# A graph network with an eigensolver on one core: a norm's small steps moved from VectorE to GpSimd, and a residual add made by a copy and an accumulating DMA

## The chip, the core and the metric

The kernel runs on one core of one Trainium2 chip. The core has five engines with a queue each: TensorE (PE; its weight loads are PEld), VectorE (DVE), ScalarE (ACT), GpSimd (POOL) and SyncE (SP, which here only issues DMAs). An engine takes its instructions in the order of the program; a semaphore wait at the head of a queue holds all that stands behind it. The metric is the time in microseconds of one execution on the device. One execution of each kernel was also taken by the hardware profiler.

## The reference, cut to what matters

x has 64 batches of 256 rows and 256 features; adj is 256 x 256. All is float32.

```python
h = maximum(layernorm(x), 0)                    # layer 0
g = adj * adj
t = relu(g @ (h @ W1))                          # 256 -> 512, per batch
t = relu(g @ (t @ W2))                          # 512 -> 1024
x = x + g @ (t @ W3)                            # 1024 -> 256
h = maximum(layernorm(x), 0)                    # layer 1
L = normalised laplacian of adj
U = eigenvectors of L (eigh)
h = relu((U.T @ h) @ W1' + b1)                  # 256 -> 128
x = x + U @ (h @ W2' + b2)                      # 128 -> 256
```

with `layernorm(x) = (x - mean) / sqrt(var + 1e-5)` over the features.

## The kernel before, in words

Two jobs run beside each other. The **eigen chain** (class `Eigen`) finds U: a Householder reduction to tridiagonal form of 254 steps, 16 small QL problems, four merge levels (32, 64, 128, 256). Almost all of it is small VectorE instructions that depend on each other, with a square root on ScalarE, transposes on TensorE and, in the first half of the reduction, up to nine small instructions of a step on GpSimd (named m, q, qn, qs, none, gg, gu, xc in the profile; `aside` chooses GpSimd while `lo < P` and VectorE after it; m and none stay on GpSimd to the end).

**Layer 0** (class `Layers`) has no need of U. It goes over 32 pairs of batches. For pair q: `begin` loads x (two DMAs of 256 KB) and makes `norm` and `relu_norm`, which give h0; `first` to `fourth` are the matrix products, whose results ScalarE takes out of PSUM; `last` multiplies with g once more and adds x, which gives x1, a tile of 128 partitions x 1024 (two 128 x 512 halves, m = 0 and 1). x1 of the first 30 pairs is spilled to DRAM by SyncE, that of the last two is kept (`KEPT = 2`). `norm1` normalises x1 into h1, `turn_rows` transposes it, `for_layer1` multiplies it with the first weight of layer 1 and spills the product.

A float32 product appears in the trace as two matmul instructions.

`norm` takes for each of the four rows of a partition: a Copy on ScalarE with a running sum, one VectorE instruction for minus the mean (nm), a Square on ScalarE with a running sum (v); then for the four together one VectorE scaling of v, a square root on ScalarE, a reciprocal, a correction step of three, a reciprocal and the shift, all on VectorE. In all seven small VectorE instructions. `relu_norm` applies scale and shift in four ScalarE instructions.

**Layer 1** (`layer1`) needs U and goes over the pairs again, in three stages of a software pipeline (`to_vectors`, `from_vectors`, `finish`), twelve products in all for a pair. GpSimd adds x1 and the bias product (xb, two instructions of 128 x 512 for a pair).

The **order** on every engine is fixed when the program is built, by a planner (`Pace`). It keeps a clock for each engine and a price for each instruction (`Op`: `busy` is how long the engine is taken, `until` when the result can be read). The eigen chain is written out in its own order; before each of its instructions, `Pace.chain` asks when that instruction is due and `Pace.run` puts in front of it those instructions of the two layer-0 streams (`products` and `rows`) which by their prices start earlier. A matmul that would go past the due time is cut in two. Chain instructions are priced 6% longer than their nominal price (13% while the QL problems run), layer-0 ones at their nominal price. So TensorE is given layer-0 products until the chain's next transposes are due, and real times that differ from the prices show up as waits at the head of a queue.

The two streams are each in order. `rows` gives begin(0), begin(1), norm1(0), begin(2), norm1(1) and so on. `products` gives, for pair q: third(q), turn_rows(q-1), half of fourth(q), for_layer1(q-1), first(q+1), the other half of fourth(q), second(q+1), last(q). norm1(q) thus has third(q+1) to hide under. The last pair's turn_rows waits until layer 1 says so: layer 1 starts with the planner weaving what is left of layer 0 between its own instructions (there one layer-0 product goes ahead of about each layer-1 product), and when it comes to its ninth pair (`LAST_AT = 12`, three pairs ahead) everything left of layer 0 is put in at once (`pace.finish`), since pairs 30 and 31 come twelfth and thirteenth in its order.

The small pools matter for the edit: x has two buffers, x1 two, and the PSUM pool of layer 0 has four banks, which `bank()` hands out in turn.

In the profile nearly every instruction carries line 209, the line of the planner that issues it (213 when the planner no longer weaves), so the tiles tell what an instruction is. `x<-x,bank` is the residual add, `junk<-x` a Copy of a norm, `junk<-x,nm` its Square, `s<-v` its square root, `h<-x,shift,scale` relu_norm, `s<-bank` and `y<-bank` evictions of products, `p<-bank` one of fourth, `p,gt` the products of last, `gt,h` those of first, `eye,h` those of turn_rows, `ident,ac` the chain's transposes. x1 and x are one name in it, and so are `L_gnn_W` of both layers.

Of the kernel before, what the change touches and what calls it, by code (L numbers as in the profile page):

```python
# [21 lines left out]
F32 = mybir.dt.float32  # L22
AF = mybir.ActivationFunctionType
OP = mybir.AluOpType
# [3 lines left out]
N = 256  # L28
P = 128
# [6 lines left out]
LN_EPS = 1e-5  # L36
# [46 lines left out]
class Op:  # L83
# [4 lines left out]
    def __init__(self, part, call, args, kwargs):  # L88
        self.part, self.engine, self.call, self.args, self.kwargs = part, ENGINES[part], call, args, kwargs
        self.name = call.__name__  # L90
        free = lambda a: int(np.prod([int(n) for n in a.shape[1:]]))
        named = dict(kwargs)
        outs = [named.pop("out")] if "out" in named else [args[0]]
        ins = [a for a in [*(args if "out" in kwargs else args[1:]), *named.values()] if isinstance(a, bass.AP)]
        total = named.pop("accum_out", None)
        if isinstance(total, bass.AP):
            outs.append(total)
            ins = [a for a in ins if a is not total]
        self.outs, self.ins = [span(a) for a in outs], [span(a) for a in ins]
        n = max(free(a) for a in outs[:1] + ins) if self.engine == "DVE" else free(outs[0])  # L100
        sums = len(outs) > 1

        if self.engine == "PE":
            self.columns = 0 if "transpose" in self.name else n
            self.busy = max(n * self.COLUMN, 0.224) if self.columns else 0.115
            self.until = max(self.busy, 0.165) + 0.35
        elif self.engine == "ACT":
            pointers = any(isinstance(kwargs.get(k), bass.AP) for k in ("scale", "bias"))
            self.busy = 0.13 + n / 1400 + 0.12 * pointers + 0.19 * sums
            self.until = self.busy + 0.12  # L110
        elif self.engine == "DVE":
            each = 6.3 if self.name == "reciprocal" else 2.0 if self.name == "tensor_tensor_scan" else 1.0
            pointers = self.name == "scalar_tensor_tensor" or any(a.shape[1:] == [1] for a in ins[1:])
            self.busy = 0.065 + 0.06 * pointers + each * n / 960 + 0.08 * sums
            self.until = self.busy + 0.125
        elif self.engine == "POOL":
            self.busy = 0.2 + 2 * n / 960
            self.until = self.busy + 0.1
        else:
            self.busy, self.until = 0.1, 4.0  # L120
# [13 lines left out]
def span(a):  # L134

    step = a.ap[0][0]
    lo = a.offset % step if step else a.offset
    return a.tensor.name, lo, lo + sum((int(n) - 1) * abs(int(s)) for s, n in a.ap[1:]) + 1
# [142 lines left out]
class Eigen:  # L281
# [998 lines left out]
    def level(self, n, qt, dc, rho, sg, bad=None):  # L1280
# [93 lines left out]
        def spread(ps, column):  # L1374

            for h in range(H):
                nc.tensor.matmul(
                    ps if last else ps[:, seg[h]],
                    lhsT=column[:, h : h + 1].to_broadcast([P, P]),
                    rhs=perm[:, h, :],  # L1380
                    start=h == 0 or not last,
                    stop=h == H - 1 or not last,
                )
# [349 lines left out]
class Layers:  # L1733


    def __init__(self, tc, ctx, ap, gt2, u, ut):
        self.tc, self.nc, self.ap = tc, tc.nc, ap
        self.gt2, self.u, self.ut = gt2, u, ut
        pool = ctx.enter_context(tc.tile_pool(name="layers", bufs=1))
        self.kept = ctx.enter_context(tc.tile_pool(name="kept", bufs=KEPT))  # L1740
        dram = ctx.enter_context(tc.tile_pool(name="dram", bufs=1, space=bass.MemoryType.DRAM))
        self.x1, self.hw = {}, {}
        self.x, self.h0, self.y1, self.y2, self.s2, self.p3, self.h1, self.new = ({} for _ in range(8))
        self.begun, self.rows_of = set(), {}
        self.due = False
        self.spilled = {
            q: dram.tile([P, H * 2 * N], F32, name=f"x1_{q}") for q in range(PAIRS - KEPT)
        }
        self.spilled_hw = {
            q: dram.tile([P, H * 2 * P], F32, name=f"hw_{q}") for q in range(PAIRS - KEPT)  # L1750
        }
        self.w = {}
        for name in ("L0_gnn_W1", "L0_gnn_W2", "L0_gnn_W3", "L1_gnn_W1", "L1_gnn_W2"):
            rows, cols = ap[name].shape
            self.w[name] = pool.tile([P, rows // P, cols], F32, name=name)
        self.b1 = pool.tile([P, P], F32, name="b1")
        self.eye = pool.tile([P, P], F32, name="eye")
        self.b2 = pool.tile([P, N], F32, name="b2")
        self.u1 = pool.tile([P, H], F32, name="u1")
        self.ub2 = pool.tile([P, H, N], F32, name="ub2")  # L1760

    def load_weights(self):
        dma, ap = self.nc.sync.dma_start, self.ap
        for name, t in self.w.items():
            dma(out=t, in_=ap[name].rearrange("(c p) n -> p c n", p=P))
        dma(out=self.eye, in_=ap["c_mats"][0][0:P, 0:P])
        for b, t in (("L1_gnn_b1", self.b1), ("L1_gnn_b2", self.b2)):
            dma(out=t, in_=ap[b].rearrange("(o n) -> o n", o=1).to_broadcast(list(t.shape)))
# [42 lines left out]
    def norm(self, x, scale, shift, parts=range(4)):  # L1811

        nc = self.nc
        g = H * 2
        at = slice(parts[0], parts[-1] + 1, parts[1] - parts[0])
        s, nm, v, tmp = (self.sp.tile([P, g], F32, tag=c, name=c) for c in ("s", "nm", "v", "tmp"))
        for j in parts:
            junk = self.sp.tile([P, N], F32, tag="junk", name="junk", bufs=1)
            yield nc.scalar.activation(junk, x[:, j // 2, j % 2, :], AF.Copy, accum_out=s[:, j : j + 1])
        yield nc.vector.tensor_scalar(nm[:, at], s[:, at], -1.0 / N, None, OP.mult)  # L1820
        for j in parts:
            junk = self.sp.tile([P, N], F32, tag="junk", name="junk", bufs=1)
            yield nc.scalar.activation(
                junk, x[:, j // 2, j % 2, :], AF.Square, bias=nm[:, j : j + 1], accum_out=v[:, j : j + 1]
            )
        s, nm, v, tmp, scale, shift = (t[:, at] for t in (s, nm, v, tmp, scale, shift))

        yield nc.vector.tensor_scalar(v, v, 0.25 / N, 0.25 * LN_EPS, OP.mult, OP.add)
        yield nc.scalar.activation(s, v, AF.Sqrt)
        yield nc.vector.reciprocal(tmp, s)  # L1830
        yield nc.vector.tensor_tensor(tmp, tmp, v, OP.mult)
        yield nc.vector.tensor_tensor(s, s, tmp, OP.add)
        yield nc.vector.reciprocal(scale, s)
        yield nc.vector.tensor_tensor(shift, nm, scale, OP.mult)

    def relu_norm(self, x, scale, shift, h, parts=range(4)):
        for j in parts:
# [34 lines left out]
    def rows(self):  # L1872

        for q in range(PAIRS + 1):
            if q < PAIRS:
                if q > 0:
                    yield lambda: q - 1 in self.begun
                yield from self.begin(q)
            if q > 0:
                yield lambda: q - 1 in self.new  # L1880
                yield from self.norm1(q - 1)
# [101 lines left out]
    def last(self, q):  # L1983

        nc, x, p3 = self.nc, self.x.pop(q), self.p3.pop(q)
        x1 = self.kept.tile([P, H, 2, N], F32, tag="x1", name="x1")
        for m in range(H):
            ps = self.bank()
            yield from self.products_of(ps, [(self.gt2[:, h, m * P : (m + 1) * P], p3[:, h, :]) for h in range(H)])
            yield nc.vector.tensor_tensor(flat(x1)[:, m, :], flat(x)[:, m, :], ps, OP.add)  # L1990
        if q in self.spilled:
            yield nc.sync.dma_start(out=self.spilled[q], in_=x1.rearrange("p h b f -> p (h b f)"))
        else:
            self.x1[q] = x1
        self.new[q] = x1
# [137 lines left out]
def flat(t):  # L2133
    return t.rearrange("p h b f -> p h (b f)")
# [63 lines left out]
```

## Time and profile before

| | us |
|---|---|
| median of 3 runs (2427.26 to 2429.52) | 2429.36 |
| span of the profiled execution | 2426.6 |
| TensorE idle before layer-0 products that wait for ScalarE (s), whole run | 6.5 |
| ScalarE idle before relu_norm, waiting for shift, 50 times | 54.4 |
| ScalarE idle before the square root of a norm, waiting for v, 47 times | 36.8 |
| ScalarE idle before Square, waiting for nm, 42 times | 32.6 |
| GpSimd idle before m, waiting for the eigen chain's xr, 250 times | 526.5 |
| DMA queue of SyncE, share of 16 engines | 10.8% |

TensorE's clock was granted in full (0.999 on the mean). The longest chain of work that the profile follows back from the end starts only at 2247.6 us, where U is done; from there it is TensorE's products of layer 1 with one pair's norm in front. The rest of the reading is in the prediction, with its lines.

How to read the views: a group's row has the operation, the tiles out<-in, the shapes, the count, then busy us and mean ns of one, then idle time before it and who ended it. A row of a tile's view has the count and the shortest, median and longest duration in ns. A row of waits has the total us, the number of times and the longest. A row of the timeline has the start, the length, the engine, the operation and, in brackets, the idle time before it.

### The profile page before, as it was taken

The numbers are of one execution on the slowest core, as the hardware profiler recorded it, in microseconds if no ns is written. First come the engines' busy times: TensorE is split into PE (matmuls) and PEld (weight loads), VectorE is DVE, ScalarE is ACT, GpSimd is POOL, SyncE is SP. The second block draws the span as 40 slices with busy tenths as digits, with TensorE's granted clock in tenths as the row PEclk, the third lists the DMA queues.
The fourth block names the chain that finished last, engine by engine and source line by source line (L and its number), as shares of the span: only waits on it lengthen the run. The fifth ranks groups of instructions, "written<-read, shape, count | busy, mean of one in ns | idle before, by whom it ended". The sixth has DMA issues, their size and how long they took to land. (4 is left out here: it accounts for less than half of the span.)

```text
span 2426.6 us, 38393 instructions
## 1 busy us (share of the span) xinstructions
PE 2381.5 (98%) x9226; PEld 1581.7 (65%) x9226; DVE 2127.2 (88%) x12971; ACT 1013.8 (42%) x2827; POOL 480.6 (20%) x1752
## 2 busy tenths in 40 slices
PE   7999999999999999999999899999999999999999
PEld 4666666666666566666666666666566666666788
DVE  8999999999999999999999989999997888886443
ACT  4444454444444444344444244344344434443322
POOL 2334333343333111111111000000000000000443
PEclk9999999999999999999999999999999999999999
DMA  3000000000000000000000000000000000000676
GB/s 113 18 21 7 23 23 18 23 23 23 6 23 23 18 22 23 22 6 23 23 23 26 10 23 23 23 23 22 18 22 27 22 23 12 16 22 1 210 255 204
DMA packets 59399, 90.02 MB, mean 37 GB/s; under 512 B 5792, under 2 KB 42784, under 8 KB 59168
## 3 DMA queue, kind: packets, MB, share of 16 engines
q1 hardware_dynamic: 59168, 87.52, 10.8%
q8 instruction: 74, 1.21, 0.2%
q14 instruction: 157, 1.29, 0.2%
HBM read 47.13 MB, written 40.37 MB: 36 GB/s over the span
## 5 line engine op out<-in xcount | busy, mean ns | idle before, releaser
L209 PE MATMUL bank<-y,L_gnn_W 128*128 128x512 f32 (+2 forms) x2182 | 903.5, 566 | 1.1 <-ACT y L209 1.1
L209 PEld LDWEIGHTS bank<-y,L_gnn_W 128*128 128x128 f32 x2182 | 401.8, 190 | 440.7 <-issue 419.0
L209 PE MATMUL bank<-L_gnn_W,s 128*128 128x256 f32 (+1 forms) x2092 | 465.2, 375 | 3.2 <-ACT s L209 3.2
L209 PEld LDWEIGHTS bank<-L_gnn_W,s 128*128 128x128 f32 x2092 | 386.7, 190 | 52.2 <-ACT s L209 3.9
L209 ACT ACTIVATE s<-bank 128x512 f32<-128x512 f32 x384 | 224.9, 586 | 196.4 <-PE bank L209 196.0
L209 PE MATMUL bank<-gt,s 128*128 128x256 f32 x1036 | 233.7, 379 | 2.8 <-ACT s L209 2.8
L209 PE MATMUL bank<-L_gnn_W,y 128*128 128x512 f32 (+2 forms) x542 | 230.9, 569 | 1.1 <-ACT y L209 1.1
L209 PEld LDWEIGHTS bank<-gt,s 128*128 128x128 f32 x1036 | 194.7, 191 | 39.7 <-issue 10.5
L209 ACT COPY y<-bank 128x512 f32<-128x512 f32 x192 | 111.5, 582 | 138.9 <-PE bank L209 138.6
L209 PEld LDWEIGHTS bank<-L_gnn_W,y 128*128 128x128 f32 x542 | 100.2, 190 | 97.3 <-issue 91.1
L209 POOL COPY m<-xr 128x1 f32<-128x1 f32 x254 | 55.8, 220 | 534.5 <-DVE xr L209 526.5
L209 ACT ACTIVATE s<-nn,guard 128x1 f32<-128x1 f32 x254 | 74.5, 293 | 208.1 <-DVE nn L209 169.0
L209 ACT ACTIVATE h<-x,shift,scale 128x256 f32<-128x256 f32 x256 | 137.3, 589 | 54.6 <-DVE shift L209 54.4
L209 ACT ACTIVATE junk<-x 128x256 f32<-128x256 f32 x256 | 105.6, 412 | 95.8 <-DVE x L209 80.5
L209 ACT ACTIVATE junk<-x,nm 128x256 f32<-128x256 f32 x256 | 129.0, 504 | 37.1 <-DVE nm L209 32.6
L209 DVE SCALAR_TENSOR_TENSOR A<-xr,wc,A 128x255 f32<-128x255 f32 (+63 forms) x381 | 139.9, 368 | 0.0
L209 DVE SCALAR_TENSOR_TENSOR A<-wr,q,A 128x255 f32<-128x255 f32 (+63 forms) x381 | 138.9, 366 | 0.0
L209 ACT ACTIVATE junk<-xr 128x254 f32<-128x254 f32 (+63 forms) x127 | 46.0, 362 | 216.5 <-DVE xr L209 211.4
L209 DVE SCALAR_TENSOR_TENSOR q<-q 128x1 f32<-128x1 f32 (+1 forms) x576 | 119.8, 208 | 13.0 <-ACT q L209 2.3
L209 PE MATMUL bank<-gt,h 128*128 128x256 f32 (+1 forms) x518 | 120.6, 382 | 0.1
L209 POOL TENSOR_TENSOR xb<-x,ub 128x512 f32<-128x512 f32 x16 | 19.9, 1271 | 495.5 <-DMA hw<-hw 485.6
L209 PE MATMUL bank<-p,gt 128*128 128x512 f32 (+2 forms) x270 | 117.0, 570 | 0.1
(615 smaller groups left out, 4306.2 us busy)
## 6 DMA issues: line engine op xcount, KB each, us to landing
x<-x SPq DMA_DIRECT2D x60, 512.0 KB, 3.6
x<-in_x_dram SPq DMA_DIRECT2D x64, 256.0 KB, 3.7
out_dram<-out SPq DMA_DIRECT2D x64, 256.0 KB, 2.2
hw<-hw SPq DMA_DIRECT2D x60, 256.0 KB, 2.7
L_gnn_W<-in_L_gnn_W_dram SPq DMA_DIRECT2D x1, 2048.0 KB, 10.9
L_gnn_W<-in_L_gnn_W_dram SPq DMA_DIRECT2D x1, 1024.0 KB, 13.5
L_gnn_W<-in_L_gnn_W_dram SPq DMA_DIRECT2D x1, 512.0 KB, 6.3
mask<-in_c_blk_dram SPq DMA_DIRECT2D x2, 256.0 KB, 3.1
```

The lines of the kernel that those rows point to most:

```text
L209: return op.call(*op.args, **op.kwargs)
```

## The change

Two edits and a price. In `norm` the Copy is scaled by -1/N, so that its running sum is nm at once; the square root takes v with its scale and the epsilon as a bias, from a new constant tile `eps`; one reciprocal r stays on VectorE, and one Newton step for 1/sqrt (w = 1.5 - 0.5 v r r, scale = r w) and the shift are six GpSimd instructions. In `last` ScalarE copies both PSUM banks into x1, and then a DMA issued by GpSimd adds x to x1 in SBUF; the spill and norm1 read x1 after it. The planner gets a price for a DMA on GpSimd: 1.1 us of the engine, result after 5.0 us.

```diff
+        elif self.engine == "POOL" and "dma" in self.name:
+            self.busy, self.until = 1.1, 5.0
         elif self.engine == "POOL":
             self.busy = 0.2 + 2 * n / 960
...
+        self.eps = pool.tile([P, 1], F32, name="eps")
+        self.nc.vector.memset(self.eps, LN_EPS)
...
     def norm(self, x, scale, shift, parts=range(4)):
...
         for j in parts:
             junk = self.sp.tile([P, N], F32, tag="junk", name="junk", bufs=1)
-            yield nc.scalar.activation(junk, x[:, j // 2, j % 2, :], AF.Copy, accum_out=s[:, j : j + 1])
-        yield nc.vector.tensor_scalar(nm[:, at], s[:, at], -1.0 / N, None, OP.mult)
+            yield nc.scalar.activation(
+                junk, x[:, j // 2, j % 2, :], AF.Copy, scale=-1.0 / N, accum_out=nm[:, j : j + 1]
+            )
...
-        yield nc.vector.tensor_scalar(v, v, 0.25 / N, 0.25 * LN_EPS, OP.mult, OP.add)
-        yield nc.scalar.activation(s, v, AF.Sqrt)
-        yield nc.vector.reciprocal(tmp, s)
-        yield nc.vector.tensor_tensor(tmp, tmp, v, OP.mult)
-        yield nc.vector.tensor_tensor(s, s, tmp, OP.add)
-        yield nc.vector.reciprocal(scale, s)
-        yield nc.vector.tensor_tensor(shift, nm, scale, OP.mult)
+        yield nc.scalar.activation(s, v, AF.Sqrt, scale=1.0 / N, bias=self.eps)
+        yield nc.vector.reciprocal(r, s)
+        yield nc.gpsimd.tensor_scalar(w, v, 1.0 / N, LN_EPS, OP.mult, OP.add)
+        yield nc.gpsimd.tensor_tensor(w, w, r, OP.mult)
+        yield nc.gpsimd.tensor_tensor(w, w, r, OP.mult)
+        yield nc.gpsimd.tensor_scalar(w, w, -0.5, 1.5, OP.mult, OP.add)
+        yield nc.gpsimd.tensor_tensor(scale, r, w, OP.mult)
+        yield nc.gpsimd.tensor_tensor(shift, nm, scale, OP.mult)
...
     def last(self, q):
...
-            yield nc.vector.tensor_tensor(flat(x1)[:, m, :], flat(x)[:, m, :], ps, OP.add)
+            yield nc.scalar.copy(flat(x1)[:, m, :], ps)
+        rows = lambda t: t.rearrange("p h b f -> p (h b f)")
+        yield nc.gpsimd.dma_start(out=rows(x1), in_=rows(x), accum_op=OP.add)
```

More of the change, by code (lines that the diff above doesn't have):

```diff
@@ L1815, in norm @@
         at = slice(parts[0], parts[-1] + 1, parts[1] - parts[0])
-        s, nm, v, tmp = (self.sp.tile([P, g], F32, tag=c, name=c) for c in ("s", "nm", "v", "tmp"))
-        for j in parts:
-            junk = self.sp.tile([P, N], F32, tag="junk", name="junk", bufs=1)
-            yield nc.scalar.activation(junk, x[:, j // 2, j % 2, :], AF.Copy, accum_out=s[:, j : j + 1])
-        yield nc.vector.tensor_scalar(nm[:, at], s[:, at], -1.0 / N, None, OP.mult)
+        nm, v, s, r, w = (self.sp.tile([P, g], F32, tag=c, name=c) for c in ("nm", "v", "s", "r", "w"))
         for j in parts:
@@ L1823, in norm @@
             yield nc.scalar.activation(
-                junk, x[:, j // 2, j % 2, :], AF.Square, bias=nm[:, j : j + 1], accum_out=v[:, j : j + 1]
+                junk, x[:, j // 2, j % 2, :], AF.Copy, scale=-1.0 / N, accum_out=nm[:, j : j + 1]
             )
-        s, nm, v, tmp, scale, shift = (t[:, at] for t in (s, nm, v, tmp, scale, shift))
-        yield nc.vector.tensor_scalar(v, v, 0.25 / N, 0.25 * LN_EPS, OP.mult, OP.add)
-        yield nc.scalar.activation(s, v, AF.Sqrt)
-        yield nc.vector.reciprocal(tmp, s)
-        yield nc.vector.tensor_tensor(tmp, tmp, v, OP.mult)
-        yield nc.vector.tensor_tensor(s, s, tmp, OP.add)
-        yield nc.vector.reciprocal(scale, s)
-        yield nc.vector.tensor_tensor(shift, nm, scale, OP.mult)
+        for j in parts:
+            junk = self.sp.tile([P, N], F32, tag="junk", name="junk", bufs=1)
+            yield nc.scalar.activation(
+                junk,
+                x[:, j // 2, j % 2, :],
+                AF.Square,
+                bias=nm[:, j : j + 1],
+                accum_out=v[:, j : j + 1],
+            )
+        nm, v, s, r, w, scale, shift = (t[:, at] for t in (nm, v, s, r, w, scale, shift))
+        yield nc.scalar.activation(s, v, AF.Sqrt, scale=1.0 / N, bias=self.eps)
[6 more added lines that the diff above has]
+        yield nc.gpsimd.tensor_tensor(shift, nm, scale, OP.mult)
     def relu_norm(self, x, scale, shift, h, parts=range(4)):
```

## The prediction

> **What bounds the kernel now.** I read the busy shares first, then the busy times of four stretches, then the gaps before TensorE's instructions, then the rows of the operations that move.
>
> ```profile
> PE 2381.5 (98%) x9226; PEld 1581.7 (65%) x9226; DVE 2127.2 (88%) x12971; ACT 1013.8 (42%) x2827; POOL 480.6 (20%) x1752
> ...
> 0.00:60.00 60.00, 45.38 (x152) 26.69 (x153) 48.01 (x239) 29.14 (x85) 16.89 (x63) 1.00 0.36 115
> 60.00:1320.00 1260.00, 1252.21 (x4948) 817.22 (x4947) 1210.75 (x7701) 570.37 (x1653) 375.76 (x1590) 1.00 0.06 20
> 1320.00:2247.00 927.00, 911.41 (x3331) 588.40 (x3329) 794.70 (x4926) 367.80 (x1001) 8.03 (x36) 1.00 0.06 19
> 2247.00:2426.60 179.60, 172.47 (x798) 149.35 (x798) 73.69 (x108) 46.51 (x88) 79.91 (x64) 1.00 0.68 226
> ```
>
> The columns of the stretches are start:end, length, then busy us of PE, PEld, DVE, ACT and POOL. TensorE is idle for 2426.6 - 2381.5 = 45.1 us: 14.6 before 60, 7.8 during the tridiagonal reduction (60 to about 1320), 15.6 in the leaves and merge levels, 7.1 in layer 1. Layer 0 fills TensorE while the eigen chain runs on VectorE; both are nearly full, but only TensorE's work is of fixed size at the end. When the chain ends (about 2247) layer 0 is used up to its last product, so neither runs far ahead. That a busy TensorE is at its pace shows in one row:
>
> ```profile
> 2195.03 23.77 PE L209 MATMUL bank<-y,L_gnn_W 128*128 128x512 f32 x56
> ```
>
> 56 matmuls in 23.77 us are 0.424 us each. The 256-wide ones of layer 1 come 8 in 1.73 us, 0.216 each, the same per column. So a shorter VectorE queue gains nothing by itself; only the 45.1 us of gaps can be won, and only some. The Trainium skill, "Perfetto Trace Analysis", section "Identifying the Most-Contended Engine", warns that matmul busy time says little of the headroom and that weight-load busy time (65% here) says more; by that rule VectorE's relief would come through and the time would fall by far more than I forecast. The spacing of 0.424 us disagrees with it for this kernel.
>
> **What goes from VectorE.** Two groups:
>
> ```profile
> L209 DVE TENSOR_TENSOR x<-x,bank 128x512 f32<-128x512 f32 x64 | 43.4, 678 | 0.7 <-PE bank L209 0.6
> ...
> L209 DVE TENSOR_SCALAR v<-v 128x4 f32<-128x4 f32 x63 | 11.1, 177 | 12.9 <-ACT junk L209 12.3
> L209 DVE TENSOR_SCALAR nm<-s 128x4 f32<-128x4 f32 x63 | 11.1, 176 | 7.4 <-ACT junk L209 6.8
> ...
> L209 DVE RECIPROCAL scale<-s 128x4 f32<-128x4 f32 x63 | 10.8, 172 | 0.3
> ```
>
> The 64 adds are 43.4 us. Of a norm's seven small operations six leave: 11.1 + 11.1 + 10.8 + 10.8 + 10.6 + 10.4 = 64.8 us (1.03 per norm). Together 108.2 us, and about 20 us of waits of VectorE for ScalarE's sums (12.3 + 6.8). TensorE's total is untouched, so on the path this is 0, except where a late VectorE operation stops ScalarE and thereby TensorE. These gaps are in the timeline of TensorE after 1440 (last bracket: idle before, and who ended it):
>
> ```profile
> 1487.23 7.17 PE L209 MATMUL bank<-L_gnn_W,s 128*128 128x256 f32 x32 [0.83 <-ACT s L209]
> 1553.75 7.17 PE L209 MATMUL bank<-L_gnn_W,s 128*128 128x256 f32 x32 [1.66 <-ACT s L209]
> 1715.56 4.97 PE L209 MATMUL bank<-gt,s 128*128 128x256 f32 x14 [2.40 <-ACT s L209]
> 1753.02 7.17 PE L209 MATMUL bank<-L_gnn_W,s 128*128 128x256 f32 x32 [0.72 <-ACT s L209]
> ...
> 2251.32 1.97 PE L209 MATMUL bank<-hw,u 128*128 128x256 f32 x8 [1.57 <-ACT junk L209]
> 2253.72 1.99 PE L209 MATMUL bank<-hw,u 128*128 128x256 f32 x8 [0.43 <-DMA hw<-hw]
> 2256.19 1.99 PE L209 MATMUL bank<-ut,s 128*128 128x256 f32 x8 [0.47 <-ACT s L209]
> ```
>
> The first four are 5.6 us; at 1553 a norm's chain stood ahead of the eviction, at 1715 a square root of the eigen chain. I count half, **-2.8 us** (bounds 0 and -5.6). The last three, 2.5 us, are there because layer 0 has run out when layer 1 starts. With a shorter chain some layer-0 work is left to fill them: **-2.5 us** (bounds 0 and -2.5).
>
> **What comes to ScalarE.** 64 copies of a PSUM bank at 0.582 us (the row p<-bank has 64 in 37.2) are 37 us on an engine that is 42% busy. On the path: a pair's norm starts after copy and transfer, not after the add. In the pair at 600 us the add ended at 602.3, h1 was done at 613.5 and TensorE turned it at 631.6; h0 of the next pair was done at 624.9 and first used at 642.2. That is 17 us of cover; 0.6 + a transfer of 5.4 (below) fit in. The first pass of the norm loses its VectorE step; the tail grows by five dependent GpSimd steps (gg to gu start 0.27 apart, so 1.35 us) against five VectorE steps about 0.2 apart. Cost 0 under the same cover; without it 0.4 x 64 = 26 us.
>
> **What comes to GpSimd.** 6 x 65 = 390 small operations. The nearest rows run from gg at 0.195 to q at 0.444; none<-none,nn at 0.285 takes 111 us (bounds 76 and 173) on an engine 20% busy before. What it does to VectorE shows in two places:
>
> ```profile
> L209 DVE TENSOR_SCALAR gc<-ac,z 128x2 f32<-128x2 f32 x127 | 32.5, 256 | 0.4
> ...
> L209 DVE TENSOR_SCALAR gc<-ac,z 128x1 f32<-128x1 f32 x127 | 26.2, 207 | 0.0
> ...
> L209 DVE TENSOR_TENSOR s<-s,tmp x65: 101/156/1191, 11.9 to 2260.6; 128x4 f32<-128x4 f32 x63, 128x2 f32<-128x2 f32 x2
> ```
>
> gc takes 0.05 us longer in the half where GpSimd's gg runs beside it (though on two columns), and a norm's s<-s,tmp took up to 1.191 us; the slow ones fall after 2253, where GpSimd makes adds of 1.27 us. So a GpSimd operation can hold VectorE for up to its own length. Per norm VectorE loses 1.03 us of work and gets back 6 x 0.05 = 0.3 to 6 x 0.285 = 1.71. The nearer row is gc (an operation of the same size): net relief, path 0. At the other end the chain is 0.68 us late per norm, less some 0.2 of slack per step (VectorE idles 49 us in 254 steps); 36 norms before 1320 make +17 us. The Trainium skill, "SBUF — State Buffer", section "SBUF: two separate sides", says that VectorE and GpSimd lock one port pair for whole instructions, which agrees with the 1.191. It adds that a DMA issued by GpSimd waits for its descriptors, 620 ns growing to 3100. No run here shows that; by it each transfer would land 2.5 us later than I take.
>
> GpSimd also issues 32 DMAs. Its issue cost is not in the trace; SyncE's issues take 0.32 to 1.28 us, median 0.48 for the x loads. The issue waits for ScalarE's second copy, and behind it stand the eigen chain's gg, gu, q, qn, qs, none, which VectorE's f, den and nb need. Half of these leave GpSimd at half of the reduction, after some ten pairs. (0.48 - 0.2 of slack) x 10 = **+2.8 us** (0 to 11). After 1320 GpSimd has 8 us of work in 927.
>
> **The accumulating transfer.** It reads x and x1 and writes x1, 512 KB each. Nearest is the spill of the same tile, 3.0 at the least and 3.6 in the median, which moves two such streams: 3.6 x 3/2 = 5.4. Bounds: 3.0, and 8.1, the longest landing of any x tile. The planner places its readers 5.0 after the issue. Who waits: SyncE's spill, and behind it the next x loads (17 us of cover); and ScalarE's first Copy of norm1, with the chain's Square and square root and third's evictions behind it. An overrun is stood already:
>
> ```profile
> ACT junk L209 <- DVE x L209: 80.5, 40, 6.8
> ```
>
> ScalarE waits 2.0 us on average, 40 times, at this very place and TensorE has no gap there. So 0.4 late costs 0; the point from which it decides is a landing of 7.0.
>
> **Sum.** -2.8 - 2.5 + 2.8 = -2.5 us on a span of 2426.6, so 2424.1; the median of the runs, 2429.4, lies 2.8 above that span, so **2427 us**. A difference under 0.2% (5 us) can't be told from none.
>
> **Rivals.** *TensorE was not the limit after all*: VectorE's relief removes the gaps of the reduction and levels. For it: VectorE's 96% share to 1320. Against: a gap-free TensorE. At best 7.8 + 15.6 + 2.5 = 25.9 us: 2403. It decides where those 23 us of gaps are VectorE's lateness and not the planner's order.
>
> *The transfer lands late* (slower). Place: ScalarE's first Copy of each norm1. If it lands at 8.1, ScalarE stands 1.1 us beyond what is borne, the chain's square root behind it, and TensorE at the chain's transposes: 1.1 x 32 = 35, 2462; at 7.5 it is 2443, at 9 it is 2491. For it: VectorE is busy nearly always and GpSimd must issue beside it. Against: the 17 us of cover and the DMA engines' share of 0.06.
>
> *The tail comes uncovered* (slower). The order is fixed by the planner, which now ends the chain earlier. The relief of up to 108 us is 1.5 pairs (the turns of h1 are 71 us apart, 560.7 and 631.6). Layer 1's first eight pairs carry this leftover along; what doesn't fit is put before the ninth in one block, and then the last pair's norm stands alone: 2249.0 to 2266.1 is 17 us, with the transfer 22, of which I take 17: 2444. Against: up to the ninth pair layer 1 has 84 products ((8 + 7 + 6) x 4), and the planner sets about one product of layer 0 (two matmuls of 0.424) before each: room for some 71 us.
>
> **How the numbers follow.** Forecast 0.50, with its own range 2416 to 2438 (all bounds of its small terms, few at once): 0.18 faster, 0.20 the same, 0.12 slower. TensorE not the limit 0.14, late transfer 0.21, tail 0.15. Sums: faster 0.32, same 0.20, slower 0.48: one single likeliest case near nothing, and two mishaps on one side. The range 2410 to 2466 leaves out about half of the first rival and a third of the second, under 0.2.
>
> **What would show it.** TensorE busy within a few us of 2381; VectorE about 100 lower; ScalarE 37 higher; GpSimd 110 to 150 higher; gaps at 2251 to 2256 gone. The transfer's landing against 5.0 and 7.0, and a wait of ScalarE's norm for DMA x1, tell of the second rival; a TensorE gap after the last p,gt product, of the third; TensorE gaps before ident,ac under 1320, of a chain held by GpSimd. I am wrong if TensorE's busy time itself moves by more than 10 us.

## The result, and the profile after

The changed kernel takes 2518.89 us (median, 2516.71 to 2522.43), the kernel before, run beside it, 2429.44 (2427.26 to 2430.41): a ratio of 1.0372, with an interval of 1.0358 to 1.0386. It is slower by 90 us, where 2427 was forecast.

First TensorE's line of the page and the stretches of the changed kernel, with the same bounds as before (columns: start:end, length, busy us of PE, PEld, DVE, ACT, POOL, then the granted clock, the DMA share, GB/s).

```profile
PE 2407.2 (96%) x9176; PEld 1587.8 (63%) x9176; DVE 2058.9 (82%) x12518; ACT 1057.6 (42%) x2891; POOL 591.2 (23%) x2174
...
0.00:60.00 60.00, 46.62 (x147) 26.65 (x148) 47.31 (x228) 29.37 (x85) 21.29 (x82) 1.00 0.36 115
60.00:1320.00 1260.00, 1197.92 (x4660) 777.85 (x4659) 1182.65 (x7496) 557.37 (x1594) 430.20 (x1804) 0.98 0.09 26
1320.00:2247.00 927.00, 911.49 (x3289) 581.44 (x3288) 764.28 (x4702) 399.95 (x1073) 65.73 (x219) 1.00 0.11 32
2247.00:2516.20 269.20, 251.18 (x1083) 201.87 (x1081) 64.65 (x96) 70.94 (x139) 73.97 (x70) 0.97 0.41 138
```

The span grew by 2516.2 - 2426.6 = 89.6 us, and two numbers hold it. TensorE is idle for 109.0 us in place of 45.1 (+63.9), and busy for 2407.2 in place of 2381.5 (+25.7) with the same work. The idle time came in two places: 60 to 1320, the reduction, went from 7.8 to 62.1 us (+54.3), and the end from 7.1 to 18.0 (+10.9). The leaves and merge levels have 15.5 where they had 15.6. The busy time came with the clock: the 0.98 and 0.97 are short stretches in which it was granted at half.

What a gap of the reduction looks like is in the timeline of all engines, at the end of one pair's `last` (start, length, engine, operation; in brackets the idle time before and its releaser):

```profile
104.94 0.81 PE L211 MATMUL bank<-p,gt 128*128 128x384 f32 x2
...
105.79 0.59 ACT L211 COPY x<-bank 128x512 f32<-128x512 f32 x1 [1.58 <-PE bank L211]
...
106.69 1.07 POOL L211 DMA_DIRECT2D x<-x  x1 [1.65 <-ACT x L211]
...
110.81 0.66 PE L211 MATMUL psB<-ident,ac 128*128 128x128 f32 x2 [5.06 <-DVE xr L211]
...
111.43 0.34 SPq L211 DMA_DIRECT2D x<-x  x1
111.46 0.42 ACT L211 ACTIVATE junk<-x 128x256 f32<-128x256 f32 x1 [2.98 <-DMA x<-x]
...
111.69 1.06 PE L211 MATMUL bank<-y,L_gnn_W 128*128 128x512 f32 x1
```

After the last product of `last` TensorE has nothing for 5.06 us but to wait for the chain's next transposes; the products of the next `third` (y,L_gnn_W) come only behind these, in the same place as SyncE's spill, 4.7 us after the transfer's issue. In the kernel before, the same row starts 0.65 us after the last product does:

```profile
106.09 0.81 PE L209 MATMUL bank<-p,gt 128*128 128x384 f32 x2
106.74 6.60 PE L209 MATMUL bank<-y,L_gnn_W 128*128 128x512 f32 x16
```

The chain wasn't late there: its transposes start at 104.50 and 110.81, one step of 6.3 us, in which VectorE is nearly full (5.6 of the 6 us from 106 to 112). The releaser in the bracket (xr) is only who ended the gap. The question is why the products of `third`, which read nothing of x1, stood behind the transposes. TensorE's waits of the whole run:

```profile
PE psB L211 <- DVE xr L211: 54.1, 26, 5.1
PE bank L211 <- ACT h L211: 14.9, 4, 12.9
```

The first was 3.9 us before. The second is the end: the last pair's norm stands alone in front of TensorE.

```profile
2358.47 3.68 PE L211 MATMUL bank<-p,gt 128*128 128x512 f32 x8
2375.10 0.47 PE L211 MATMUL bank<-eye,h 128*128 128x128 f32 x1 [12.95 <-ACT h L211]
2376.08 1.82 PE L211 MATMUL bank<-eye,h 128*128 128x128 f32 x7 [0.51 <-ACT h L211]
```

### The profile page after: what moved, and what is told of

It is laid out like the page before. It is cut to its first block, busy times and chain, and to the rows that moved or that the text cites. A ratio compares the mean times of both kernels' runs of the same rounds, so it can differ in the third digit from the quotient of the medians.

```text
span 2516.2 us, 38383 instructions
## 1 busy us (share of the span) xinstructions
PE 2407.2 (96%) x9176; PEld 1587.8 (63%) x9176; DVE 2058.9 (82%) x12518; ACT 1057.6 (42%) x2891; POOL 591.2 (23%) x2174
## 5 line engine op out<-in xcount | busy, mean ns | idle before, releaser
L211 PE MATMUL bank<-y,L_gnn_W 128*128 128x512 f32 (+2 forms) x2154 | 929.5, 582 | 1.6 <-PEq L1731 1.2
L211 PE MATMUL bank<-gt,s 128*128 128x256 f32 (+1 forms) x1036 | 232.6, 377 | 0.4 <-ACT s L211 0.3
L211 PE MATMUL bank<-L_gnn_W,y 128*128 128x512 f32 (+3 forms) x536 | 230.9, 574 | 1.1 <-ACT y L211 1.1
L211 PE MATMUL psB<-ident,ac 128*128 128x128 f32 x381 | 87.1, 284 | 62.6 <-DVE xr L211 54.1
L211 PEld LDWEIGHTS psB<-ident,ac 128*128 128x128 f32 x381 | 47.6, 138 | 129.1 <-issue 93.7
L211 ACT ACTIVATE junk<-x 128x256 f32<-128x256 f32 x256 | 105.4, 412 | 55.2 <-DMA x<-x 42.5
L211 POOL DMA_DIRECT2D x<-x x32 | 29.5, 921 | 402.3 <-ACT x L211 339.0
```

What stands on the lines that cost most here:

```text
L211: return op.call(*op.args, **op.kwargs)
```

## The experiments

The theory after this reading: nothing in the hardware makes `third` wait. `last` yields the spill in the stream of products, ahead of the next `third`. The planner prices the transfer's result at 5.0 us, so the spill isn't due before that, the stream's head blocks what is behind it, and TensorE gets no product until the chain's transposes. The rivals: a transfer, a copy or a GpSimd issue that is itself too slow, or GpSimd's small norm steps holding the chain.

All medians below are of runs beside the kernel before, whose own medians on these chips were 2427.4 (e1 to e4), 2428.8 (e5 to e8) and 2426.3 (e9 to e11).

**One half of the change each.** e1 is the changed kernel with `last` as it was (the norm's edit alone), e2 the changed kernel with `norm` as it was (the x1 edit alone).

```diff
# e1
-            yield nc.scalar.copy(flat(x1)[:, m, :], ps)
-        rows = lambda t: t.rearrange("p h b f -> p (h b f)")
-        yield nc.gpsimd.dma_start(out=rows(x1), in_=rows(x), accum_op=OP.add)
+            yield nc.vector.tensor_tensor(flat(x1)[:, m, :], flat(x)[:, m, :], ps, OP.add)
# e2
-        yield nc.gpsimd.tensor_scalar(w, v, 1.0 / N, LN_EPS, OP.mult, OP.add)
...
+        yield nc.vector.tensor_scalar(v, v, 0.25 / N, 0.25 * LN_EPS, OP.mult, OP.add)
...
```

> Only the norm's edit; x1 is made by VectorE as before. Theory A (the spill, planned 5 us after the transfer's issue, stands in the products' stream and lets TensorE run dry before the chain's next transposes): no gaps like those of the changed kernel between 60 and 1320, TensorE idle there 7 to 15 us instead of 62, and a time of 2425 to 2445, the upper part if the last pair's norm stands uncovered in the tail. Theory B (GpSimd's small operations and waits hold the eigen chain): gaps before ident,ac remain, 2470 or more.

> Only the copy and the accumulating transfer; the norm stays on VectorE. Theory A: nearly all of the loss is here, TensorE idle 50 to 65 us between 60 and 1320 and a time of 2485 to 2515. Theory B: without the norm's GpSimd operations most of the loss goes, 2430 to 2450.

e1 measured 2421.39 us, ratio 0.9973 (0.9964 to 0.9983): a small gain. e2 measured 2523.8, ratio 1.0399 (1.0382 to 1.0417), with TensorE busy for 1198.51 us of the reduction and a gap of 12.57 at the end. Each lies outside theory A's range, on the side away from theory B's. The x1 edit has all of the loss and the norm's edit none: GpSimd's norm steps don't hold the chain long enough to cost time on the whole.

**The spill out of the products' way.** e3 is the changed kernel with one line in another stream: the spill is yielded by `norm1`, in `rows`, and no longer by `last`. The transfer, its price and all work stay.

```diff
     def last(self, q):
-        if q in self.spilled:
-            yield nc.sync.dma_start(out=self.spilled[q], in_=x1.rearrange("p h b f -> p (h b f)"))
-        else:
+        if q not in self.spilled:
             self.x1[q] = x1
...
     def norm1(self, q):
+        if q in self.spilled:
+            yield self.nc.sync.dma_start(out=self.spilled[q], in_=x1.rearrange("p h b f -> p (h b f)"))
```

> The changed kernel, but the spill of x1 is issued by the stream of rows ahead of norm1 instead of by the stream of products. All operations and the transfer's landing stay. Theory A: TensorE idle between 60 and 1320 falls from 62 us to under 15, the low-clock stretches that follow the gaps go too; 2435 to 2455, with the tail's gap of 13 us left. Theory B, and the theory that the transfer itself lands late: no change, 2510 to 2525.

It measured 2416.61 us, ratio 0.9954 (0.9937 to 0.9970), 102 us under the changed kernel and faster than the kernel before. Its stretches, and its timeline of TensorE at the place shown above:

```profile
60.00:1320.00 1260.00, 1254.70 (x4995) 822.88 (x4993) 1206.10 (x7604) 587.82 (x1687) 435.62 (x1821) 1.00 0.10 28
1320.00:2247.00 927.00, 916.11 (x3331) 590.18 (x3332) 746.06 (x4604) 388.05 (x1036) 66.42 (x212) 1.00 0.11 33
2247.00:2414.60 167.60, 162.92 (x757) 141.47 (x755) 61.35 (x90) 44.14 (x84) 69.28 (x61) 1.00 0.63 209
```

```profile
106.11 0.81 PE L211 MATMUL bank<-p,gt 128*128 128x384 f32 x2
106.76 5.31 PE L211 MATMUL bank<-y,L_gnn_W 128*128 128x512 f32 x12
111.97 0.40 PE L211 MATMUL psB<-ident,ac 128*128 128x128 f32 x2
```

`third` follows `last` at once, the reduction's idle time is 5.3 us, and the gap at the end is gone too (4.7 us idle after 2247). I had expected that gap to stay, hence the 2435 to 2455; it was a consequence. The transfer lands 4.6 us after its issue as before (median of 32), and ScalarE waits for it 20 times, 29.4 us in all; TensorE's longest wait for the chain's xr before the transposes is now 0.6 us, where it was 5.1.

**The price alone.** e4 is the kernel *before*, with only the planner's number for the residual add on VectorE raised. No operation differs from the kernel before; only the order does.

```diff
-            yield nc.vector.tensor_tensor(flat(x1)[:, m, :], flat(x)[:, m, :], ps, OP.add)
+            add = nc.vector.tensor_tensor(flat(x1)[:, m, :], flat(x)[:, m, :], ps, OP.add)
+            add.until = 5.6
+            yield add
```

> The kernel before, with one number of the planner changed: the residual add on VectorE is planned to be readable 5.6 us after its start. No operation differs, only the order. Theory A: gaps of 3 to 5 us before the chain's transposes appear in the reduction, 40 to 65 us of TensorE idle between 60 and 1320, and with the lower clock after them 2480 to 2510. Theory B and the theory of the late transfer: nothing to hold anything, 2429 +- 8.

It measured 2508.3 us, ratio 1.0332 (1.0314 to 1.0349), with TensorE busy for 1204.49 us of the reduction and the same kind of gap:

```profile
319.69 0.66 PE L209 MATMUL psB<-ident,ac 128*128 128x128 f32 x2 [4.07 <-DVE xr L209]
```

81 us are lost without a transfer, a copy or a GpSimd instruction added. A planned wait alone is enough.

**Controls for the move.** e5 is the kernel before with the spill moved as in e3. e6 is e2 with the spill moved (the x1 edit alone, in the good order). e7 is e3 with the accumulating DMA moved to `norm1` as well.

```diff
# e7, norm1 (in last the same line is gone)
...
+        yield self.nc.gpsimd.dma_start(out=rows(x1), in_=rows(self.old.pop(q)), accum_op=OP.add)
         if q in self.spilled:
```

> The kernel before with only the spill of x1 moved, from last (products stream) to the head of norm1 (rows stream). A control for e3. If the spill hurts only because of the 5.0 us price of the transfer ahead of it, there is nothing to win here, where the spill stands behind a VectorE add that is priced 0.7 us: 2424 to 2430, TensorE idle between 60 and 1320 still about 8 us. If the move were a gain of its own, which e3 had on top of the change, this kernel would come out near 2420 or under.

> The x1 edit alone (norm as before), with the spill moved to norm1. If the planned order was its whole cost (e2: 2523.8), the gaps before the chain's transposes go and the time falls to 2418 to 2432; the copies of ScalarE and the 32 transfers then cost nothing. If the copies, the transfer or GpSimd's issues cost something by themselves, part of the 94 us stays: over 2440.

> The changed kernel with the accumulating DMA and the spill both moved to the head of norm1. The products stream then holds nothing that waits: TensorE idle between 60 and 1320 at 5 to 8 us as in e3, the time 2411 to 2420. Under 2412 would say that the DMA's place in the products stream still cost something in e3; over 2420 that the transfer is now late for the norm.

e5 measured 2431.68 us, ratio 1.0015 (1.0006 to 1.0024): the move is no gain of its own (and 1.7 us over the range given). e6 measured 2424.15, ratio 0.9983 (0.9974 to 0.9992): with the order mended, 64 copies on ScalarE and 32 transfers cost nothing on the whole. Its reduction has 10.6 us of TensorE idle against 6.5 in e5; the cause of these 4 us stays open, as VectorE waits for GpSimd's qs no longer than in e5 (1.3 us against 1.5). e7 measured 2417.79, ratio 0.9953 (0.9940 to 0.9967), level with e3: once the spill is out of the products, the place of the transfer's issue doesn't matter.

**A lower price, which didn't go as expected.** If the price is to blame, why not lower it? e8 has 1.7 us for the transfer's result in the changed kernel.

```diff
-            self.busy, self.until = 1.1, 5.0
+            self.busy, self.until = 1.1, 1.7
```

> The changed kernel with one number of the planner changed: the result of a DMA on GpSimd is priced 1.7 us after its issue instead of 5.0; the transfer itself still lands after 4.6. If the planned order is the cause, TensorE gets its products again and the time falls to 2418 to 2445, the upper part if ScalarE now has to wait up to 3 us more at the Copy of 32 norms. If the real transfer or its issue is the cause, nothing goes: 2500 or more.

It measured 2501.27 us, ratio 1.0295 (1.0281 to 1.0309), which is neither: the "price alone" theory was too simple. TensorE's gaps were shorter (no gap before the transposes over 2.4 us), but ScalarE's wait for the transfer went from 42.5 us in 20 times to 140.9 in 32. Two kernels split this. e9 is e4 with 2.4 us, about what e8's planner sees between the last product and the spill, and no transfer that could be late. e10 is e8 with 0.3 us, so that the planner sees no wait at all.

> As e4 (the kernel before, with another planner price for VectorE's residual add and nothing else), but 2.4 us in place of 5.6: as much as e8's planner sees from the last product to the spill. No transfer, so nothing can be late. e8 was 2501, with 36 us more TensorE idle in the reduction, 18 more in the levels, 140.9 us of ScalarE waiting for the transfer. If the low price still starves TensorE by plan, the reduction's idle here is as in e8 (40 to 48 us), the levels' as before (15 to 20), the time 2460 to 2480. If what remained in e8 was the real transfer on ScalarE, this kernel is near the one before: idle in the reduction under 20, time 2428 to 2445.

> As e8 with the price of the transfer's result at 0.3 us. The planner then sees no wait, so no planned starvation; the transfer still lands 4.6 us after its issue, and ScalarE meets it at the first Copy of norm1 with the chain's Square behind it. If the real lateness alone is dear (my rival of a late transfer, reached through the price): 2470 to 2510, with ScalarE's waits for the transfer at 140 to 190 us and TensorE's gaps only in the steps after it. If only the planned order costs: 2418 to 2440.

e9 measured 2433.33 us, ratio 1.0032 (1.0021 to 1.0043): a planned wait of 2.4 us costs only some 7 us. e10 measured 2517.75, ratio 1.0376 (1.0358 to 1.0393), as slow as the changed kernel and 8 us over the range expected, with the wait now in the hardware. Its waits of ScalarE, and its timeline of one pair:

```profile
ACT junk L211 <- DMA x<-x: 158.6, 32, 7.4
```

```profile
255.03 0.94 POOL L211 DMA_DIRECT2D x<-x  x1
...
256.10 0.38 PE L211 MATMUL psB<-ident,ac 128*128 128x128 f32 x2
...
259.72 0.42 ACT L211 ACTIVATE junk<-x 128x256 f32<-128x256 f32 x1 [4.99 <-DMA x<-x]
...
262.39 0.37 ACT L211 ACTIVATE junk<-xr 128x217 f32<-128x217 f32 x1
...
262.94 0.27 POOL L211 TENSOR_SCALAR none<-m 128x1 f32<-128x1 f32 x1 [3.23 <-ACT junk L211]
...
264.58 0.40 PE L211 MATMUL psB<-ident,ac 128*128 128x128 f32 x2 [2.30 <-DVE ac L211]
```

The norm's Copy heads ScalarE's queue for 4.99 us, and three Copies more and a Square go ahead of the chain's Square (junk<-xr). GpSimd's none waits 3.23 us for that, and the chain's step, transposes to transposes, takes 8.5 us in place of 6.3. So the transfer's time has to be paid for by a plan that puts other work there: told of it in the wrong stream, the planner lets TensorE run dry; not told, it lets the chain stand. e8 has both: by e9 the planned wait would be worth some 7 of its 73 us, so most of them go with ScalarE's waits, though no run took these away from e8.

**The end.** e11 is the changed kernel with the last two pairs later in layer 1's order (`LAST_AT = 20` in place of 12), so that the leftover of layer 0 has more to lie under.

> The changed kernel with the last two pairs put 20th and 21st in layer 1's order in place of 12th and 13th, so that what is left of layer 0 has eight more pairs of layer 1 to lie under. If the tail's gap of 12.95 us and the half clock after it (17.1 us at half, some 8 us) are a consequence of the leftover: 2495 to 2506, no gap over 2 us after 2247. If the tail is not what I take it for: 2515 to 2522.

It measured 2501.07 us, ratio 1.0309 (1.0292 to 1.0326), 18 us under the changed kernel. TensorE is full where the 12.95 us gap was, and at the full clock (the granted clock is the third number from the end):

```profile
2247.00:2376.00 129.00, 129.00 (x528) 95.81 (x527) 17.66 (x27) 34.99 (x70) 22.29 (x24) 1.00 0.29 90
```

So 15 (by the ratios) to 18 of the 90 us are the uncovered tail with its half clock, and the rest is the reduction. No run took only the half clock away; that its 25.7 us belong to the gaps rests on the places of the half-clock stretches and on e3, which has a single half-clock stretch, of 3.4 us, and 2380.1 us of TensorE busy.

## Why the prediction was wrong, by its own steps

- **The step that failed** is in what comes to ScalarE: "That is 17 us of cover; 0.6 + a transfer of 5.4 fit in", and with it the list of who waits for the transfer: SyncE's spill with the next x loads, and ScalarE's first Copy. The cover is real in the hardware, and e3 has it. But it consists of the next `third`, and the spill stood ahead of `third` in the same planned stream. I listed the spill as a waiter on SyncE's queue and didn't ask which stream it heads in the planner. Both facts were in the text ahead of the prediction: the order of `products`, and a price of 5.0 us for the result. It cost 54 us of idle time in the reduction, the larger part of 25.7 in clock, and 10.9 at the end.
- **TensorE as the bound** held, and was the reason why the loss shows so fully: its gaps pass into the span (in e3 they are 10.6 us less than before, and the span is 12.0 less). "I am wrong if TensorE's busy time itself moves by more than 10 us" came true with 25.7. I hadn't reckoned with the clock.
- **VectorE's relief** was put at 108.2 us and measured 68.3 (2127.2 to 2058.9). The instructions did leave (12971 to 12518), and none of the costliest rows that stayed moved by more than 0.2 us; small instructions overlap with their neighbours (at 110.32, 110.45 and 110.58 us three of 0.21 us each start, den, ac and xr), so a sum of rows overstates what the busy time loses. On the path I gave it 0 plus 5.3 us in small gaps. In the good order the whole change gains 11 us (e3, against its kernel before); TensorE's idle time falls by 1.0 before 60, 2.5 in the reduction, 4.7 in the levels and 2.4 in layer 1, the last as forecast (2.5). The gaps behind evictions (s), from which I took 2.8, fell only from 6.5 us to 5.3, so most of what the levels gained lay in other gaps. The forecast gain in gaps, 5.3, was about half of the 10.6 that came, and the 25.9 of the first rival were far off.
- **GpSimd's small steps** were too dear in my sum: 0.285 us taken, 0.208 to 0.231 measured, 85 us in all for the 111 taken. That GpSimd's busy time rose by 110.6 is luck: the 32 issues, 0.92 us each (0.48 taken), make up the difference. For the issues I charged 2.8 us of the path. The eigen chain's waits for GpSimd did grow, but with the norm's steps and not with the issues: VectorE's idle time for qs went from 1.1 us to 5.2; in e1, which issues no DMA on GpSimd, it is 6.2, and in e6, which issues all 32, only 1.3. Of contention, given 0, VectorE's gc shows none: 256 ns as before.

```profile
L211 POOL TENSOR_TENSOR w<-w,r 128x4 f32<-128x4 f32 x126 | 28.4, 226 | 63.5 <-DVE r L211 25.0 <-DVE q L211 20.0 <-DVE c L211 4.6
L211 POOL TENSOR_SCALAR w<-v 128x4 f32<-128x4 f32 x63 | 14.6, 231 | 251.5 <-ACT junk L211 241.7 <-ACT rdq L211 8.8
```

```profile
L211 DVE TENSOR_SCALAR gc<-ac,z 128x2 f32<-128x2 f32 x127 | 32.5, 256 | 0.1
```

  VectorE's row that waits for qs, in the kernel before, in e1 and in e6:

```profile
L209 DVE SCALAR_TENSOR_TENSOR m<-rs,qn,qs 128x1 f32<-128x1 f32 x254 | 55.2, 217 | 9.9 <-POOL qs L209 1.1
...
L211 DVE SCALAR_TENSOR_TENSOR m<-rs,qn,qs 128x1 f32<-128x1 f32 x254 | 55.1, 217 | 14.6 <-POOL qs L211 6.2
...
L211 DVE SCALAR_TENSOR_TENSOR m<-rs,qn,qs 128x1 f32<-128x1 f32 x254 | 55.3, 218 | 10.2 <-POOL qs L211 1.3
```

- **The transfer** was taken at 5.4 us and landed in 4.6, under the planner's 5.0 and the deciding point of 7.0. The second rival (late transfer, 2462) was thus not what happened in the changed kernel. Its mechanism is true, as e10 shows, once the plan leaves no room.

```profile
x<-x POOLq DMA_DIRECT2D x32, 512.0 KB, 4.6
```

  The Trainium skill, "SBUF — State Buffer", section "SBUF: two separate sides", was weighed in the prediction with descriptors that come some 2.5 us late; the page measured that beside a VectorE tensor_copy. Here VectorE is busy for 94% of the reduction with other operations, and nothing points to such a wait: 4.6 us less 2.5 would leave 2.1 for the transfer, and the spill, which moves fewer streams, takes 3.4 in the same run.
- **The uncovered tail** (2444) did occur, with a gap of 12.95 us. I expected it from a chain that ends early; what made it was layer 0 left behind by the starved reduction. In the changed kernel layer 1's first product of U comes at 2223.1, 28 us sooner than in the kernel before; in e3 it comes at 2203.7, 48 us sooner, and yet the tail is covered.

## What to carry to other kernels

Where a planner fixes the order, a longer latency is paid at the head of the stream in which the *reader* of the result is listed, so look at what is listed behind that reader before counting hardware cover. If the work that should hide a transfer stands behind the transfer's first reader, move the reader (here one spill) to the stream that can afford to wait; lowering the price only moved the loss here from a starved TensorE to a stalled chain. A planner's price can be tested by itself, in a kernel where no operation changes.

## What the hardware showed beside this

After its longer gaps TensorE's clock was granted at half, for 3.4 us or a multiple of it. The stretches around the first gap shown (105.75 to 110.81), with the granted clock third from the end:

```profile
106.00:108.00 2.00, 0.00 (x0) 0.00 (x0) 2.00 (x8) 0.87 (x3) 1.31 (x3) 1.00 0.00 0
108.00:110.00 2.00, 0.00 (x0) 0.00 (x0) 1.77 (x9) 0.29 (x1) 1.66 (x6) 0.91 0.93 178
110.00:112.00 2.00, 1.19 (x5) 1.22 (x6) 1.87 (x13) 0.51 (x2) 0.39 (x2) 0.50 0.45 84
...
116.00:118.00 2.00, 2.00 (x6) 0.93 (x5) 1.68 (x11) 0.29 (x1) 0.59 (x3) 0.88 0.00 0
```

The clock falls some 3.9 us after TensorE stopped and comes back at about 116.4, 5.6 us after it started again; the products in between run at half pace (those of 512 columns start 0.85 us apart, in place of 0.424). The changed kernel has 13 such stretches, 81.9 us in all, the kernel before two of 3.4. So this gap of 5.1 us cost, by this working, 5.1 + 5.6 / 2 = 7.9. After the 12.95 us gap at the end the half clock lasts 17.1 us.

The Trainium skill, "TensorE: Matmul & The Clock Gate", section "HAM oscillation — how this bites in real kernels", states that idle gaps over some 3.4 us halve the clock and that every burst after such a gap starts slow. The 3.4 us is here the unit of the half-clock stretches. As a bound for a gap it doesn't agree: in e10 the gap of 2.30 us shown above (262.28 to 264.58) was followed by half clock from 266.0 to 269.4, when TensorE was at work again:

```profile
264.00:266.00 2.00, 1.42 (x7) 0.97 (x8) 1.70 (x12) 1.90 (x7) 0.58 (x3) 0.99 0.01 4
266.00:268.00 2.00, 2.00 (x4) 0.85 (x3) 1.97 (x9) 0.08 (x1) 1.42 (x4) 0.50 0.01 4
```

It is no single case. All 17 such stretches of e10 follow gaps of 2.3 to 5.3 us, eleven of them under 3.2. In the kernel before, the gap of 2.40 us that the prediction shows in front of 1715.56 is followed by half clock from 1716.5 to 1719.9.
